# A graph network's node matrix as one float32r product of 258 columns, b2 read from memory, and a new order of the steps

## The chip, the cores and the metric

The kernel runs on one core of a Trainium2 chip. The metric is the device time of one launch in microseconds (us). The engines are named as the profile names them: PE (TensorE, matrix products; PEld is its loading of weights), DVE (VectorE), ACT (ScalarE), POOL (GpSimd) and SP, whose queue issues most DMAs. Each engine runs its own instructions in the order in which they were written.

## The reference

There are 128 graphs of 128 nodes with 512 features. For each graph, `adj` is a 128 x 128 matrix. Two layers follow one another; only what this case touches is shown in full.

```python
# layer 0: h = relu(layernorm(x));  x = x + (hconv(layernorm(relu(hconv(h, adj, W1, b1))), adj, W2, b2) + h)
def hypergraph_conv(x, adj, W, b):
    H = (adj != 0).astype(x.dtype)
    w = adj.reshape(N, -1)[:, :C]                    # adj's first row
    xw = jnp.einsum('ncd,hd->nch', x, W)
    Dn = jnp.einsum('nce,ne->nc', H, w)
    Dn = jnp.where(Dn > 0, 1.0 / Dn, 0.0)
    Be = H.sum(axis=1)
    Be = jnp.where(Be > 0, 1.0 / Be, 0.0)
    m = Be[:, :, None] * jnp.einsum('nce,nch->neh', H, xw)
    out = Dn[:, :, None] * jnp.einsum('nce,neh->nch', H, m)
    return out + b
# layer 1: h = relu(layernorm(x));  agg = adj @ h / max(row sums of adj, 1e-6)
#          x = x + relu(concat(h, agg) @ W.T)
```

All is float32. The hidden width of layer 0 is 1024 (W1 is 1024 x 512, W2 is 512 x 1024).

## The kernel before

A graph's 128 nodes lie on the 128 partitions. The H ... B ... H^T of the hypergraph convolution is one 128 x 128 **node matrix** per graph, S = H diag(1/Be) H^T, and the same product yields Dn, because the weights w (adj's first row) stand beside the scaled H as one more column. `incidence` transposes adj by blocks on DVE (`adjt`), writes the weight column into `sb`, turns adjt into zeros and ones while counting them, and takes the reciprocal of the count; `incidence_scale` writes the 128 scaled columns into `sb`; `node_matrix` (L402 to L408) multiplies `adjt` by `sb`, 128 x 129 columns in plain float32, and ACT evicts the sum to `s`; `node_scale` (L411 to L420) makes 1/Dn and its multiples from the last column, in four or five DVE instructions of one column (tile `dinv`).

The large products are made in float32r, which the program feeds with operands split in two parts: a high part `h` (a copy rounded down by a factor) and a low part `l` (the difference), and a third part `d` for a correction. `product` (L480 to L496) therefore runs three sweeps into two PSUM banks, called main (`rm`, `gm`, `bm`, `am`) and correction (`rd`, `gd`, `bd`, `ad`). Per graph these are conv1 in two halves (tiles `rm`, `rd`, twice), conv2 (`gm`, `gd`), the mean part of layer 1 (`bm`, `bd`) and its self part (`am`, `ad`). Small products are `ps_s` (node matrix), `pz` (conv1's nodes, float32), `ym` and `yd` (conv2's nodes, split as well) and the aggregation (L791).

The program is a software pipeline: `head` starts it, `step(s)` runs for s = 3 to 124, and `tail` ends it. Within a step the calls stand in an order written out by hand in the source, and every stage names its graph relative to s: `node_matrix(s + 1)`, `conv1_weights(s, 1)`, `conv2_nodes(s - 2)`, `layer1_mean(s - 3)` and so on. Nothing else schedules: an engine's queue is this order, filtered by engine. "Steady" graphs (3 to 120) take some other forms than those of head and tail.

Names used later. `conv1_out` (L514, DVE) adds a correction bank to `r`; `conv1_bias` (L519, POOL, pieces of 256 columns at L81) adds b1; `inner_*` is the layer norm of 1024 columns; `inner_out` and `inner_in` write r to DRAM and read it back in blocks (`n_scratch`, `nb`), `inner_turn` (L550) transposes the blocks into `nt`, which is split into `nh`, `nl`, `nd`. `layer1_trip_out`, `layer1_trip_in`, `layer1_turn`, `layer1_high`, `layer1_low`, `layer1_rest` do the same for layer 1 (`h_scratch`, `hb`, `ht`, `hh`, `hl`, `hd`). `mean_operator`, `mean_scale`, `mean_out`, `mean_in`, `mean_transpose` normalise adj by its row sums, and take it through DRAM (`an_scratch`, `anb`). `residual` (L436) adds h to x on POOL and then, for a steady graph, adds b2 with an accumulating DMA that POOL issues (`moved`, L91), from a copy of b2 on all partitions (`b2_bc`). `conv2_out` (L713) adds `ym` and `yd` to x. `scales` and `shifts` are the one-column instructions of the layer norms. Many tiles have one buffer: `r`, `adj`, `sb`, `ht`.

Of the kernel before, what the change touches and what calls it, by code (L numbers as in the profile page):

```python
# [24 lines left out]
def gnn_kernel(  # L25
# [34 lines left out]
    P = 128  # L60
# [99 lines left out]
    b2_bc = const.tile([P, D], FP, name="b2_bc")  # L160
# [171 lines left out]
    SB, HT, S, DN, H0, Z, PZ, SPLIT = ({} for _ in range(8))  # L332

    @stage
    def mean_operator(g):

        a = ADJ.pop(g)
        deg = small.tile([P, 1], FP, tag="deg", name="deg", bufs=2)
        nc.vector.tensor_reduce(deg, a, AX.X, ADD)
        nc.vector.tensor_scalar(deg, deg, EPS_DEG, 1.0 / 4096.0, MAX, MUL)  # L340
        nc.vector.reciprocal(deg, deg)
        ADJ[g] = a, deg
# [37 lines left out]
    @stage  # L380
    def incidence(g):


        HT[g] = at = pool.tile([P, P], FP, tag="ht", name="adjt")
        nc.vector.transpose(at, ADJB.pop(g))
        SB[g] = sb = small.tile([P, P + 1], FP, tag="sb", name="sb")
        nc.vector.tensor_scalar(sb[:, P : P + 1], at[:, 0:1], DOWN_12, None, MUL)
        cnt = small.tile([P, 1], FP, tag="cnt", name="cnt", bufs=2)
        nc.vector.tensor_scalar(at, at, 0.0, None, ALU.not_equal, ADD, accum_out=cnt)

        nc.vector.tensor_scalar(cnt, cnt, 1.0, None, MAX)
        nc.vector.reciprocal(cnt, cnt)
        SB[g] = sb, cnt

    @stage
    def incidence_scale(g, eng):
        SB[g], cnt = SB[g]
        scaled(eng, SB[g][:, :P], HT[g], cnt)


    @stage
    def node_matrix(g):  # L402
        ps = small_bank("ps_s")
        nc.tensor.matmul(ps[:, : P + 1], HT.pop(g), SB.pop(g), start=True, stop=True)  # L404
        s = small.tile([P, P + 1], FP, tag="s", name="s", bufs=4)
        copy(s, ps[:, : P + 1], AF.Copy, scale=4096.0 if steady(g) else 1.0)  # L406
        S[g] = s[:, :P]
# [3 lines left out]
    def node_scale(g):  # L411
        w = DN[g]
        DN[g] = dn = small.tile([P, 4], FP, tag="dinv", name="dinv", bufs=6)
        inv = dn[:, 2:3]
        nc.vector.tensor_scalar(inv, w, TINY, None, MAX)
        nc.vector.reciprocal(inv, inv)
        nc.vector.scalar_tensor_tensor(dn[:, 0:1], w, 0.0, inv, ALU.is_gt, MUL)
        nc.vector.tensor_scalar(dn[:, 1:2], dn[:, 0:1], ONE_UP, None, MUL)
        if not steady(g):
            nc.vector.tensor_scalar(dn[:, 3:4], dn[:, 0:1], DOWN_12, None, MUL)  # L420
# [15 lines left out]
    def residual(g, eng=nc.gpsimd):  # L436
        combine(eng, X[g], X[g], H0[g], ADD)
        if steady(g):
            moved(X[g], b2_bc)
        else:  # L440
            combine(eng, X[g], X[g], b2_bc, ADD)
# [373 lines left out]
    def step(s):  # L815
        node_high(s - 2)
        layer1_high(s - 3)
        conv2_bias(s - 2)
        inner_out(s - 1)
        inner_in(s - 1)  # L820
        conv2_high(s - 2)
        node_rest(s - 2)
        node_matrix(s + 1)
        mean_out(s - 3)
        layer1_low(s - 3, nc.vector)
        layer1_self_main(s - 4)
        conv1_weights(s, 1)
        mean_in(s - 3)
        conv2_low(s - 2, nc.vector)
# [3 lines left out]
        finish(s - 4)  # L833
        load_adj(s - 2)
        layer1_rest(s - 3)
        x_norm(s + 1)
        conv1_main(s, 0)
        conv2_out(s - 2)
        store(s - 4)
        conv1_nodes(s + 1)  # L840
        conv1_main(s, 1)
        conv1_out(s, 1)
        conv1_out(s, 0)
        conv1_high(s + 1)
        conv1_bias(s, 1)
        layer1_mean(s - 3)
        inner_turn(s - 1)
        layer1_sums(s - 2)
        conv1_bias(s, 0)
        conv1_low(s + 1)  # L850
        layer1_self(s - 3)
        layer1_mean_main(s - 3)
        layer1_spread(s - 2)
        load_adjb(s + 3)
        inner_high(s - 1)
        scales(s - 2, 3)
        mean_transpose(s - 3)
        shifts(s - 2, 3, nc.gpsimd)
        layer1_norm(s - 2)
        inner_sums(s)  # L860
# [583 lines left out]
```

## Time and profile before

| | us |
|---|---|
| median of 3 runs | 2458.57 (2458.56 to 2460.13) |
| the profiled execution | 2458.89 |
| its span, first to last instruction | 2457.1 |
| PE busy | 2437.2 (99%) |
| DVE busy | 2340.8 (95%) |
| ACT busy | 2061.8 (84%) |
| POOL busy | 1016.1 (41%) |

A span is what the instructions cover; 1.8 us lie around it. Busy shares are of the span. In lists of groups, the columns are line, engine, operation, tiles (output <- inputs), shape and count, then busy time in us, mean ns of one, and the engine's idle time just before with what ended it. In a list of one tile the columns are line, engine, operation, count, then the shortest, median and longest duration in ns. In a timeline they are start in us, duration in us, engine, line, operation, tiles; rows of a run of equal instructions are merged (x2, x4). In the chain, the columns are start, length and work.

### The profile page before, as it was taken

The page shows a single profiled execution, that of the slowest core. Times are in us where ns is not written, and L with a number is a line of the kernel's source. Part 1 is how long each engine was busy: PE and PEld are TensorE (multiplying, and loading weights), DVE is VectorE, ACT ScalarE, POOL GpSimd, SP SyncE. Part 2 cuts the span into 40 slices and gives each one's busy share as a digit, 9 for nine tenths or more (in the row PEclk, how much of TensorE's full clock was granted, in tenths as well). Part 3 has the DMA queues.
Part 4 walks back from the last instruction along what each step waited for, and adds up shares of the span by engine and source line. Part 5 has one row for each costly group of instructions (what it writes and reads, how often), then busy time and mean ns, then how long its engine had stood idle before and what let it go on. Part 6 is the DMA issues. An engine that isn't in the chain of part 4 may idle for free.

```text
span 2457.1 us, 41143 instructions
## 1 busy us (share of the span) xinstructions
PE 2437.2 (99%) x11300; PEld 2023.8 (82%) x11300; DVE 2340.8 (95%) x5358; ACT 2061.8 (84%) x4494; POOL 1016.1 (41%) x1560
## 2 busy tenths in 40 slices
PE   8999999999999999999999999999999999999998
PEld 6788888888888888888888888888888888888886
DVE  8899999999999999999999999999999999999987
ACT  8888888888888888888888888888888888888885
POOL 5434343444344434443444434343434343434452
PEclk9999999999999999999999999999999999999999
DMA  7454554445444544454455444544554454445432
GB/s 193 132 139 136 141 143 139 136 142 146 136 137 140 149 135 138 139 150 132 139 144 145 136 138 142 143 136 138 144 141 137 138 146 139 136 138 145 127 121 94
DMA packets 425943, 342.30 MB, mean 139 GB/s; under 512 B 178544, under 2 KB 341872, under 8 KB 425712
## 3 DMA queue, kind: packets, MB, share of 16 engines
q1 hardware_dynamic: 407888, 308.66, 41.0%
q0 software_dynamic: 17248, 30.95, 7.2%
q8 instruction: 89, 1.46, 0.3%
q14 instruction: 142, 1.16, 0.2%
q10 hardware_dynamic: 576, 0.07, 0.0%
HBM read 166.21 MB, written 142.34 MB: 126 GB/s over the span
## 4 chain that ended last, share of the span: by engine, by line
PE 83%; DVE 12%; issue 2%; ACT 2%; DMA 1%; SPq 0%; POOL 0%; DVEq 0%; ACTq 0%; POOLq 0%
PE gm L489 16%; PE rm L489 16%; PE bm L489 8%; PE am L489 8%; PE gd L494 8%; PE rd L494 8%; PE bd L494 4%; PE ad L494 4%; PE pz L447 4%; PE am L791 2%; PE ad L791 1%; DVE r L514 1%; PE ps_s L404 1%; PE yd L703 1%; PE ym L701 1%
## 5 line engine op out<-in xcount | busy, mean ns | idle before, releaser
L81 POOL TENSOR_TENSOR r<-r,b_bc 128x256 f32<-128x256 f32 x500 | 355.5, 743 | 772.5 <-DVE r L514 481.4
L303 POOL TENSOR_SCALAR st<-st 128x1 f32<-128x1 f32 x252 | 76.1, 302 | 566.9 <-DVE st L320 566.9
L460 ACT ACTIVATE z<-pz 128x512 fp32r<-128x512 f32 x128 | 76.5, 598 | 206.3 <-PE pz L447 206.3
L329 ACT ACTIVATE r<-r,st 128x1024 f32<-128x1024 f32 x128 | 159.3, 1244 | 76.7 <-POOL st L303 76.6
L81 POOL TENSOR_TENSOR g<-g,c 128x256 f32<-128x256 f32 x246 | 211.1, 1019 | 3.8 <-DVE g L653 3.8
L329 ACT ACTIVATE h<-x_t,st 128x512 f32<-128x512 f32 x255 | 206.2, 809 | 1.1 <-DVE st L303 0.4
L81 POOL TENSOR_TENSOR x_t<-x_t,h 128x256 f32<-128x256 f32 x256 | 184.7, 742 | 5.8 <-ACT h L329 5.8
L314 ACT ACTIVATE h<-x_t,st 128x512 f32<-128x512 f32 x255 | 183.5, 720 | 4.1
L514 DVE SCALAR_TENSOR_TENSOR r<-rd,dinv,r 128x512 f32<-128x512 f32 x256 | 179.8, 742 | 3.7 <-ACT r L509 1.8
L309 ACT ACTIVATE h<-x_t 128x512 f32<-128x512 f32 x255 | 159.5, 626 | 8.4 <-DVE x_t L713 5.5
L509 ACT ACTIVATE r<-rm,dinv 128x512 f32<-128x512 f32 x256 | 162.2, 690 | 4.2 <-PE rm L489 4.1
L550 DVE STREAM_TRANSPOSE nt<-nb 128x1024 f32<-128x1024 f32 x127 | 156.8, 1235 | 2.5 <-DMA nb<-n_scratch 2.5
L580 DVE SCALAR_TENSOR_TENSOR nd<-nh,nl 128x1024 fp32r<-128x1024 f32 x127 | 154.8, 1219 | 0.0
L81 DVE TENSOR_TENSOR nl<-nt,nh 128x1024 fp32r<-128x1024 f32 x126 | 152.2, 1208 | 0.0
L489 PE MATMUL rm<-w11h,z 128*128 128x512 f32 x512 | 152.0, 418 | 0.0
L489 PE MATMUL bm<-w30h,hh 128*128 128x512 f32 x504 | 146.9, 413 | 0.1
L447 PEld LDWEIGHTS pz<-s,h 128*128 128x128 f32 x1024 | 134.4, 192 | 13.7 <-ACT s L406 1.8
L314 ACT ACTIVATE junk<-r,st 128x1024 bf16<-128x1024 f32 x128 | 145.1, 1134 | 0.1
L489 PE MATMUL rm<-w11l,z 128*128 128x512 f32 x512 | 138.2, 392 | 0.0
L494 PE MATMUL rd<-w11d,z 128*128 128x512 f32 x512 | 138.0, 391 | 0.0
L447 PE MATMUL pz<-s,h 128*128 128x128 f32 x1024 | 135.9, 276 | 1.9 <-ACT s L406 1.3
L489 PE MATMUL rm<-w10h,z 128*128 128x512 f32 x512 | 137.7, 391 | 0.0
(240 smaller groups left out, 7527.0 us busy)
## 6 DMA issues: line engine op xcount, KB each, us to landing
n_scratch<-r SPq DMA_DIRECT2D x128, 512.0 KB, 2.6
nb<-n_scratch SPq DMA_DIRECT2D x508, 128.0 KB, 2.8
x_t<-in_x_dram SPq DMA_DIRECT2D x128, 256.0 KB, 2.8
h_scratch<-h SPq DMA_DIRECT2D x127, 256.0 KB, 2.0
hb<-h_scratch SPq DMA_DIRECT2D x508, 64.0 KB, 2.0
out_dram<-o SPq DMA_DIRECT2D x127, 256.0 KB, 2.1
x_t<-b_bc POOLq DMA_DIRECT2D x118, 256.0 KB, 3.7
adj_t<-in_adj_dram SPq DMA_DIRECT2D x128, 64.0 KB, 2.0
```

Of the source, the lines that this page charges most:

```text
L81: eng.tensor_tensor(dst[:, s], a[:, s], b[:, s], op)
L309: copy(junk, src, func, accum_out=t[:, 0:1])
L314: copy(junk, src, AF.Square, bias=t[:, 1:2], accum_out=t[:, 2:3])
L329: copy(dst, src, func, bias=t[:, 5:6], scale=t[:, 4:5])
L447: nc.tensor.matmul(z[:, k * P : (k + 1) * P], H0[g][:, k * P : (k + 1) * P], S[g], start=True, stop=True)
L460: copy(h, pz, AF.Copy, scale=DOWN)
L489: nc.tensor.matmul(pm, left[i](k), right(i, k), start=(i == 0 and k == 0), stop=(i == 1 and k == kk - 1))
L494: nc.tensor.matmul(pd, left[2](k), right(2, k), start=(k == 0), stop=(k == kk - 1), skip_group_check=True)
L509: copy(R[g][:, HALVES[half]], PY.pop((g, half)), AF.Copy, scale=DN[g][:, 1:2])
L514: nc.vector.scalar_tensor_tensor(r, PR.pop((g, half)), dn[:, 0:1], r, MUL, ADD)
L550: nc.vector.transpose(nt.rearrange("p k (i b) -> p k i b", b=B), t.rearrange("p i k a -> p k i a"))
L580: nc.vector.scalar_tensor_tensor(t, h, 2.0**-12, low, MUL, SUB)
```

## The change

Four things change.

1. The node matrix becomes one float32r product of 258 columns. The row factor is split: the pair (w, 1/Be) is rounded down on ACT (`incidence_high`), DVE takes the difference, and both scale the 0/1 matrix, so that `sb` holds a high half of 129 columns and a low half of 129 columns side by side. ACT evicts the first half, and a new DVE instruction (`node_sum`) adds the second from PSUM. The raw transposed adj now has a tile of its own (`raw`).
2. b2 has no copy on the partitions: the accumulating DMA reads b2's row in DRAM for every partition, and does so for all graphs.
3. Stages that were one are now several (`mean_operator`, `incidence`, `node_scale`), with an engine to be named for some one-column instructions.
4. `head`, `step` and `tail` have a new order, in which some stages also name another engine. In `step`: `layer1_low` DVE to POOL, `incidence_scale` POOL to DVE (low half) and ACT (high half), `shifts(s - 2, 3)` POOL to DVE, and the one-column instructions `node_floor` and `mean_degree` DVE to POOL, the weight column DVE to ACT.

The diff, without the orders of `head` and `tail`:

```diff
@@ -157,7 +157,6 @@
     }
 
     b1_bc = const.tile([P, DH], FP, name="b1_bc")
-    b2_bc = const.tile([P, D], FP, name="b2_bc")
     c0 = const.tile([P, D], FP, name="c0")
     gb = const.tile([P, 2, KH], FP, name="gb")
     eps = const.tile([P, 1], FP, name="eps")
@@ -329,7 +328,7 @@
         copy(dst, src, func, bias=t[:, 5:6], scale=t[:, 4:5])
 
 
-    SB, HT, S, DN, H0, Z, PZ, SPLIT = ({} for _ in range(8))
+    SB, HT, S, DN, H0, Z, PZ, SPLIT, PS = ({} for _ in range(9))
 
     @stage
     def mean_operator(g):
@@ -337,9 +336,17 @@
         a = ADJ.pop(g)
         deg = small.tile([P, 1], FP, tag="deg", name="deg", bufs=2)
         nc.vector.tensor_reduce(deg, a, AX.X, ADD)
-        nc.vector.tensor_scalar(deg, deg, EPS_DEG, 1.0 / 4096.0, MAX, MUL)
+        ADJ[g] = a, deg
+
+    @stage
+    def mean_degree(g, eng):
+        deg = ADJ[g][1]
+        eng.tensor_scalar(deg, deg, EPS_DEG, 1.0 / 4096.0, MAX, MUL)
+
+    @stage
+    def mean_inverse(g):
+        deg = ADJ[g][1]
         nc.vector.reciprocal(deg, deg)
-        ADJ[g] = a, deg
 
     @stage
     def mean_scale(g, eng):
@@ -381,43 +388,79 @@
     def incidence(g):
 
 
-        HT[g] = at = pool.tile([P, P], FP, tag="ht", name="adjt")
-        nc.vector.transpose(at, ADJB.pop(g))
-        SB[g] = sb = small.tile([P, P + 1], FP, tag="sb", name="sb")
-        nc.vector.tensor_scalar(sb[:, P : P + 1], at[:, 0:1], DOWN_12, None, MUL)
-        cnt = small.tile([P, 1], FP, tag="cnt", name="cnt", bufs=2)
-        nc.vector.tensor_scalar(at, at, 0.0, None, ALU.not_equal, ADD, accum_out=cnt)
-
-        nc.vector.tensor_scalar(cnt, cnt, 1.0, None, MAX)
-        nc.vector.reciprocal(cnt, cnt)
-        SB[g] = sb, cnt
-
-    @stage
-    def incidence_scale(g, eng):
-        SB[g], cnt = SB[g]
-        scaled(eng, SB[g][:, :P], HT[g], cnt)
-
+        raw = pool.tile([P, P], FP, tag="raw", name="raw")
+        nc.vector.transpose(raw, ADJB.pop(g))
+        HT[g] = at = pool.tile([P, P], FP, tag="ht", name="adjt").bitcast(FR)
+        two = small.tile([P, 2], FP, tag="cnt", name="cnt", bufs=2)
+        nc.vector.tensor_scalar(at, raw, 0.0, None, ALU.not_equal, ADD, accum_out=two[:, 1:2])
+
+        SB[g] = two, raw
+
+    @stage
+    def incidence_weight(g, eng):
+        two, raw = SB[g]
+        scaled(eng, two[:, 0:1], raw[:, 0:1], DOWN_12)
+
+    @stage
+    def incidence_count(g, eng):
+        two = SB[g][0]
+        eng.tensor_scalar(two[:, 1:2], two[:, 1:2], 1.0, None, MAX)
+
+    @stage
+    def incidence_inverse(g):
+        two = SB[g][0]
+        nc.vector.reciprocal(two[:, 1:2], two[:, 1:2])
+
+    @stage
+    def incidence_high(g):
+        two = SB[g][0]
+        t = small.tile([P, 2 * P + 4], FP, tag="sb", name="sb")
+        SB[g] = sb = t.bitcast(FR)
+        h, l = sb[:, P : 2 * P + 3 : P + 2], sb[:, 2 * P + 1 : 2 * P + 4 : 2]
+        copy(h, two, AF.Copy, scale=DOWN)
+        nc.vector.tensor_tensor(l, two, h, SUB)
+        SPLIT["sb", g] = t[:, 2 * P + 2 : 2 * P + 3], t[:, 2 * P + 3 : 2 * P + 4]
+
+    @stage
+    def incidence_scale(g, i, eng):
+        c = SPLIT["sb", g][i]
+        scaled(eng, SB[g][:, i * (P + 1) : i * (P + 1) + P], HT[g], c)
 
     @stage
     def node_matrix(g):
-        ps = small_bank("ps_s")
-        nc.tensor.matmul(ps[:, : P + 1], HT.pop(g), SB.pop(g), start=True, stop=True)
+        PS[g] = ps = small_bank("ps_s")
+        nc.tensor.matmul(ps[:, : 2 * P + 2], HT.pop(g), SB.pop(g)[:, : 2 * P + 2], start=True, stop=True)
         s = small.tile([P, P + 1], FP, tag="s", name="s", bufs=4)
         copy(s, ps[:, : P + 1], AF.Copy, scale=4096.0 if steady(g) else 1.0)
+        S[g] = s
+
+    @stage
+    def node_sum(g):
+        s = S[g]
+        nc.vector.scalar_tensor_tensor(s, PS.pop(g)[:, P + 1 : 2 * P + 2], 4096.0 if steady(g) else 1.0, s, MUL, ADD)
         S[g] = s[:, :P]
         DN[g] = s[:, P : P + 1]
 
     @stage
-    def node_scale(g):
+    def node_floor(g, eng):
         w = DN[g]
         DN[g] = dn = small.tile([P, 4], FP, tag="dinv", name="dinv", bufs=6)
-        inv = dn[:, 2:3]
-        nc.vector.tensor_scalar(inv, w, TINY, None, MAX)
-        nc.vector.reciprocal(inv, inv)
-        nc.vector.scalar_tensor_tensor(dn[:, 0:1], w, 0.0, inv, ALU.is_gt, MUL)
-        nc.vector.tensor_scalar(dn[:, 1:2], dn[:, 0:1], ONE_UP, None, MUL)
+        eng.tensor_scalar(dn[:, 2:3], w, TINY, None, MAX)
+        DN[g] = dn, w
+
+    @stage
+    def node_scale(g):
+        DN[g], w = DN[g]
+        dn = DN[g]
+        nc.vector.reciprocal(dn[:, 2:3], dn[:, 2:3])
+        nc.vector.scalar_tensor_tensor(dn[:, 0:1], w, 0.0, dn[:, 2:3], ALU.is_gt, MUL)
+
+    @stage
+    def node_up(g, eng):
+        dn = DN[g]
+        scaled(eng, dn[:, 1:2], dn[:, 0:1], ONE_UP)
         if not steady(g):
-            nc.vector.tensor_scalar(dn[:, 3:4], dn[:, 0:1], DOWN_12, None, MUL)
+            scaled(eng, dn[:, 3:4], dn[:, 0:1], DOWN_12)
 
     @stage
     def x_sums(g, tag="B"):
@@ -435,10 +478,7 @@
     @stage
     def residual(g, eng=nc.gpsimd):
         combine(eng, X[g], X[g], H0[g], ADD)
-        if steady(g):
-            moved(X[g], b2_bc)
-        else:
-            combine(eng, X[g], X[g], b2_bc, ADD)
+        moved(X[g], b2.partition_broadcast(P))
 
     @stage
     def conv1_nodes(g):
@@ -814,591 +854,661 @@
 
     def step(s):
         node_high(s - 2)
+        mean_out(s - 3)
+        conv2_bias(s - 2)
+        load_adj(s - 2)
+        node_rest(s - 2)
+        conv2_high(s - 2)
         layer1_high(s - 3)
-        conv2_bias(s - 2)
-        inner_out(s - 1)
-        inner_in(s - 1)
-        conv2_high(s - 2)
-        node_rest(s - 2)
         node_matrix(s + 1)
-        mean_out(s - 3)
-        layer1_low(s - 3, nc.vector)
+        layer1_low(s - 3)
+        conv2_low(s - 2, nc.vector)
+        mean_operator(s - 2)
+        node_sum(s + 1)
+        conv1_weights(s, 1)
         layer1_self_main(s - 4)
-        conv1_weights(s, 1)
-        mean_in(s - 3)
-        conv2_low(s - 2, nc.vector)
         layer1_self_out(s - 4)
         conv2_rest(s - 2)
         conv2_nodes(s - 2)
-        finish(s - 4)
-        load_adj(s - 2)
+        conv1_main(s, 0)
+        node_floor(s + 1, nc.gpsimd)
+        inner_out(s - 1)
+        inner_in(s - 1)
         layer1_rest(s - 3)
         x_norm(s + 1)
-        conv1_main(s, 0)
         conv2_out(s - 2)
-        store(s - 4)
         conv1_nodes(s + 1)
         conv1_main(s, 1)
+        layer1_sums(s - 2)
+        layer1_mean(s - 3)
+        mean_in(s - 3)
+        layer1_spread(s - 2)
         conv1_out(s, 1)
+        finish(s - 4)
+        layer1_mean_main(s - 3)
+        conv1_bias(s, 1)
+        store(s - 4)
+        inner_turn(s - 1)
+        mean_degree(s - 2, nc.gpsimd)
+        load_adjb(s + 3)
         conv1_out(s, 0)
-        conv1_high(s + 1)
-        conv1_bias(s, 1)
-        layer1_mean(s - 3)
-        inner_turn(s - 1)
-        layer1_sums(s - 2)
+        inner_high(s - 1)
         conv1_bias(s, 0)
-        conv1_low(s + 1)
-        layer1_self(s - 3)
-        layer1_mean_main(s - 3)
-        layer1_spread(s - 2)
-        load_adjb(s + 3)
-        inner_high(s - 1)
         scales(s - 2, 3)
+        shifts(s - 2, 3, nc.vector)
+        layer1_norm(s - 2)
         mean_transpose(s - 3)
-        shifts(s - 2, 3, nc.gpsimd)
-        layer1_norm(s - 2)
-        inner_sums(s)
         layer1_mean_out(s - 3)
         layer1_mean_high(s - 3)
+        node_scale(s + 1)
+        layer1_self(s - 3)
+        load_x(s + 2)
         inner_low(s - 1, nc.vector)
-        mean_rest(s - 3)
+        layer1_mean_low(s - 3, nc.vector)
+        layer1_trip_out(s - 2)
         inner_rest(s - 1)
-        layer1_mean_low(s - 3, nc.vector)
+        inner_sums(s)
+        inner_spread(s)
         layer1_mean_rest(s - 3)
-        inner_spread(s)
         scales(s, 2)
+        mean_inverse(s - 2)
         shifts(s, 2, nc.gpsimd)
         conv2_weights(s - 1)
-        layer1_trip_out(s - 2)
+        mean_rest(s - 3)
+        incidence(s + 2)
+        conv1_high(s + 1)
+        conv2_main(s - 1)
+        mean_scale(s - 2, nc.scalar)
+        incidence_count(s + 2, nc.vector)
+        conv1_low(s + 1)
+        inner_norm(s)
+        layer1_trip_in(s - 2)
+        incidence_weight(s + 2, nc.scalar)
+        x_sums(s + 2)
+        incidence_inverse(s + 2)
+        conv2_weights_out(s - 1)
+        conv1_rest(s + 1)
+        incidence_high(s + 2)
         residual(s + 1)
-        incidence(s + 2)
-        inner_norm(s)
+        x_spread(s + 2)
+        layer1_turn(s - 2)
         aggregate(s - 3)
-        node_scale(s + 1)
-        load_x(s + 2)
-        mean_operator(s - 2)
-        conv2_main(s - 1)
-        layer1_trip_in(s - 2)
-        conv2_weights_out(s - 1)
-        x_sums(s + 2)
-        x_spread(s + 2)
-        mean_scale(s - 2, nc.scalar)
-        conv1_rest(s + 1)
-        layer1_turn(s - 2)
-        incidence_scale(s + 2, nc.gpsimd)
+        incidence_scale(s + 2, 1, nc.vector)
+        incidence_scale(s + 2, 0, nc.scalar)
+        scales(s + 2, 1)
         conv1_weights(s + 1, 0)
-        scales(s + 2, 1)
         shifts(s + 2, 1, nc.vector)
+        node_up(s + 1, nc.vector)
...
```

## The prediction

> **What bounds the kernel now.** I read the busy shares first (PE 99%, DVE 95%), then the busy time in windows, which is alike from 100 us to 2300 us, so one step stands for 118 steady graphs. In the window from 1000 to 1500 us:
>
> ```profile
> 1000.00:1500.00 500.00, 500.00 (x2333) 417.60 (x2332) 484.05 (x1121) 424.26 (x932) 206.06 (x319) 1.00 0.49 141
> ```
>
> PE has no gap in 500 us at a granted clock of 1.00. Next the chain that ended last, two steps of it:
>
> ```profile
> 1216.58 0.22 PE ps_s L404 x2
> 1216.80 1.85 PE rm L489 x8
> 1218.65 0.92 PE rd L494 x4
> 1219.57 0.23 PE ym L701
> ...
> 1220.25 0.89 PE pz L447 x8
> 1221.14 1.83 PE bm L489 x8
> ...
> 1226.60 3.63 PE gm L489 x16
> ...
> 1235.44 0.22 PE ps_s L404 x2
> ...
> 1238.43 0.23 PE ym L701
> ```
>
> The reader sees PE alone, matmul after matmul. A step is 1238.43 - 1219.57 = 18.86 us. A float32r matmul of 512 columns takes 3.63 / 16 = 0.227; the node matrix, float32 with 129 columns, appears as two records of 0.11. PE is the bound.
>
> But DVE is close behind, so I read its timeline beside POOL's (POOL last, and one tile's list):
>
> ```profile
> 1212.28 0.17 DVE L416 RECIPROCAL dinv<-dinv 128x1 f32<-128x1 f32 x1
> 1212.48 0.39 DVE L417 SCALAR_TENSOR_TENSOR dinv<-s,dinv 128x1 f32<-128x1 f32 x1
> ...
> 1215.77 0.51 DVE L682 SCALAR_TENSOR_TENSOR sp<-sp,s 128x128 fp32r<-128x128 f32 x1
> 1216.20 0.28 DVE L683 SCALAR_TENSOR_TENSOR sp<-sp,s 128x128 fp32r<-128x128 f32 x1
> 1216.40 0.68 DVE L81 TENSOR_TENSOR hl<-ht,hh 128x512 fp32r<-128x512 f32 x1
> 1217.01 0.68 DVE L81 TENSOR_TENSOR gp<-g,gp 128x512 fp32r<-128x512 f32 x1
> ```
> ```profile
> 1211.42 1.43 POOL L81 TENSOR_TENSOR x_t<-x_t,h 128x256 f32<-128x256 f32 x2
> ...
> 1214.39 1.73 POOL L81 TENSOR_TENSOR g<-g,c 128x256 f32<-128x256 f32 x2
> ```
> ```profile
> L417 DVE SCALAR_TENSOR_TENSOR dinv<-s,dinv x128: 159/391/401, 20.7 to 2396.5; 128x1 f32<-128x1 f32 x128
> ```
>
> DVE instructions follow one another with no wait worth naming. Two are long for their size: L417 takes 0.39 where 0.159 is possible, and ends (1212.87) with POOL's x_t (1212.85); L682 takes 0.51 where its twin L683 takes 0.28, and ends just after POOL's g (1216.12). Both read two tiles in SBUF while POOL reads two there. I call this a **meeting**; a step before has two, 0.46 us in all.
>
> **The change part by part.** *Node matrix on PE.* Removed: 0.22. Added: one float32r matmul of 258 columns, 258/512 of 0.227 = 0.114. Bounds: 0.11 (one float32 record of half the width) and 0.227 (it might take as long as 512 columns). I take 0.114, since float32r time is set by columns in every row here that I can scale. PE loses 0.11 per step: 18.75. The eight matmuls behind a float32 product take 1.85, those among float32r 1.81; another 0.04 may go, not counted.
>
> *DVE's own work*, in distances from start to start. Removed: hl 0.61 (to POOL), the weight column L387 0.19, L415 0.17 and L340 0.18: 1.15. Moved apart: before, bl and the bd that reads it stand 0.80 apart, where two independent instructions of that size stand 0.61 apart: 0.20 saved. Three one-column results (L391, L417, L340) are no longer read by the next instruction, which costs 0.19 where an independent one costs 0.08: 0.3. Added: the low pair (128 x 2) 0.19, as a one-column instruction, bounds 0.16 and 0.39 from L417; the low half's scale 0.29 (same shape on DVE at 9.03 us); node_sum, 129 columns from PSUM, 0.30, between L683's 0.28 and L682's 0.51; one shift 0.21. Sum 0.99. Net -0.66. Own work is 18.86 - 0.46 (meetings) - 0.66 = 17.74, leaving 1.0 us per step under PE's 18.75 for meetings.
>
> *Meetings in the new order.* From the order of DVE and POOL I find four: dinv's product with conv1_bias(s, 0); the anp splits with shifts(s, 2); the low pair with conv2_bias; gp or the third part of g (L730) with hl, new on POOL (two pieces of 0.74, the row of r's bias there). Lower bound 0 each (the partner can be early), upper 0.55 (DVE's r<-r,b_bc took 1247 ns against 693 once in the tail). I take somewhat under the rows' 0.23, 0.18 each: 0.7, inside the 1.0. So hl's move costs nothing while DVE has this room; without it, all of it counts.
>
> [...]
>
> *ACT* gains the weight column and the high pair (0.20 each, as L310) and the high half's scale (0.39, as L301): 0.8. It is busy 424 of 500, 16.0 of 18.86 us, and stays under 17. *POOL* loses sb's scale (0.91) and a shift (0.28) and gains hl (1.48) and two one-column instructions (0.3 each): 206/500 x 18.86 = 7.8 becomes 8.7. Its conv1 bias starts behind `finish`, which now follows the first conv1_out and reads two SBUF tiles: up to 0.68 later, ahead of inner_sums, which ACT reaches some 0.5 later still.
>
> *b2's read.* Per transfer the same bytes. Issued at 1213.15, used by ym at 1220.06; it lands after 3.7 (median), so 3 us are free. A row of b2 read for all partitions at the start took 7.6, among loads of the same size that took 6.7 and 8.7 there; that is their queue, and I count 0. The other end, 7.6 - 6.9 = 0.7 per step, goes to the range. In head and tail 20 POOL pieces (17 us) go, off PE's path.
>
> *The queue of SP.* The new order puts r's way out (`inner_out`) behind adj's. Rows before:
>
> ```profile
> 1212.76 0.34 SPq L535 DMA_DIRECT2D n_scratch<-r  x1
> 1215.40 1.76 SPq L543 DMA_DIRECT2D nb<-n_scratch  x4
> 1217.26 0.38 SPq L535 DMA_DIRECT2D an_scratch<-adj_t  x1
> ...
> 1221.50 0.43 SPq L290 DMA_DIRECT2D adj_t<-in_adj_dram  x1
> ```
>
> From gm's end: g's eviction 0.58, adj's scale 0.39, an_scratch lands 2.5 later, only then may adj's one buffer be loaded (issue 0.43), then n_scratch lands 2.6 later and frees r's one buffer for ACT's rm (0.69), then x_norm (0.81) for pz: 8.0, with six hand-overs of 0.05 (1215.40 behind a landing at 1215.36) 8.3. PE reaches pz 1220.25 - 1211.37 - 0.11 = 8.8 after gm's end, and reads it 0.16 earlier: 0.3 spare. nb lands about 0.5 ahead of `inner_turn`. An issue is now and then 1 us late (the adj load took 1.46 at 1202.75); I put 0.02 per step for that.
>
> *Sum*, against the profiled execution (2458.9, 0.3 above the median): 118 x (0.11 - 0.02) = 10.6, ten other graphs x 0.11 = 1.1, head and tail otherwise 0 with 4 either way: 2447.2.
>
> **The rivals.** (1) *DVE becomes the bound through meetings* (slower). It decides where meetings exceed 18.86 - 17.74 = 1.1 per step. At 0.32 each, 1.28: DVE 19.02, +0.16 x 118 = 2478. For it: hl adds two POOL pieces among gp and L730. Against: deg, node_sum and o, which stand between these two, read PSUM or one tile.
> (2) *SP's longer chain stops PE before pz.* 0.3 is spare; at 0.5 late, PE loses 0.2 per step: 18.95, 2469. For it: each landing is a median, and two stand in series. Against: ACT's waits now lie elsewhere.
> (3) *No gain*: 258 columns cost as much as 512, 0.227 against 0.22, or head and tail lose what the steps gain: 2459.
>
> **How the numbers follow.** My forecast 0.58 (own range 2440 to 2453), rival 1 0.17, rival 2 0.13, rival 3 0.12. A measurement of this kernel tells 0.2% (4.9 us) from no change. Faster: nearly all of the forecast and a little of rivals 2 and 3, 0.60. Within 0.2%: 0.15, mostly rival 3. Slower: 0.25. Low end 2440: the 0.04 behind the product and 4 from head and tail; high end 2482 takes in rival 1 at its price.
>
> **What would show it.** Right: ps_s one record per graph, the next matmul 0.11 behind it; ym to ym 18.75; DVE still with no long wait, or a short one before ym; L420 and L434 on ACT without pushing pz. Wrong: idle time of PE before yd (L730 late), before pz (h or s late), or before ps_s; DVE instructions of two SBUF tiles at twice their length; ACT waiting for n_scratch before r; DVE waiting for x_t's DMA from b2.

## The result and the profile after

The changed kernel takes 2572.76 us (median of 4 runs, 2571.52 to 2575.37), the kernel before 2458.57 in the same comparison: a ratio of 1.0464, 95% interval 1.0446 to 1.0483. The change costs 114 us, where 12 us of gain were forecast.

I read first the page of the profile after (busy shares, the chain that ended last, the DMA issues with their size and median time to landing):

```profile
span 2571.2 us, 41753 instructions
...
PE 2497.2 (97%) x11170; PEld 1989.8 (77%) x11170; DVE 2369.4 (92%) x5372; ACT 2137.3 (83%) x4872; POOL 1256.2 (49%) x1787
...
PE 41%; ACT 20%; DMA 18%; DVE 11%; issue 7%; SPq 3%; POOL 0%; DVEq 0%; ACTq 0%; POOLq 0%
...
n_scratch<-r SPq DMA_DIRECT2D x128, 512.0 KB, 4.5
nb<-n_scratch SPq DMA_DIRECT2D x508, 128.0 KB, 2.8
...
x_t<-in_b_dram POOLq DMA_DIRECT2D x128, 256.0 KB, 4.4
h_scratch<-h SPq DMA_DIRECT2D x127, 256.0 KB, 2.5
...
adj_t<-in_adj_dram SPq DMA_DIRECT2D x128, 64.0 KB, 3.2
```

The same lines of the page before:

```profile
PE 83%; DVE 12%; issue 2%; ACT 2%; DMA 1%; SPq 0%; POOL 0%; DVEq 0%; ACTq 0%; POOLq 0%
...
n_scratch<-r SPq DMA_DIRECT2D x128, 512.0 KB, 2.6
...
x_t<-b_bc POOLq DMA_DIRECT2D x118, 256.0 KB, 3.7
adj_t<-in_adj_dram SPq DMA_DIRECT2D x128, 64.0 KB, 2.0
```

Before, PE was 83% of the chain and DVE 12%. Now PE is 41%, ACT 20% and transfers 18%. One landing stands out: n_scratch, r's way out, takes 4.5 us from its issue and took 2.6 before; adj's load takes 3.2 and took 2.0. Neither PE nor DVE is fuller than before: PE's share fell from 99% to 97%, DVE's from 95% to 92%.

The groups of instructions (busy time, mean ns of one, then the idle time before them and what ended it) say who waits:

```profile
L549 ACT ACTIVATE r<-rm,dinv 128x512 f32<-128x512 f32 x256 | 174.2, 682 | 156.1 <-DMA n_scratch<-r 126.6 <-DVE o L837 11.7 <-DVE s L440 11.6
...
L590 DVE STREAM_TRANSPOSE nt<-nb 128x1024 f32<-128x1024 f32 x127 | 158.0, 1244 | 68.0 <-DMA nb<-n_scratch 59.1 <-issue 8.4
...
L421 DVE TENSOR_TENSOR sb<-cnt,sb 128x2 fp32r<-128x2 f32 x128 | 143.1, 1118 | 9.3 <-ACT sb L420 5.0
...
L487 PEld LDWEIGHTS pz<-s,h 128*128 128x128 f32 x1024 | 126.5, 192 | 53.4 <-ACT h L328 49.3 <-PE pc L264 1.6 <-issue 0.5
L81 DVE TENSOR_TENSOR gp<-g,gp 128x512 fp32r<-128x512 f32 x118 | 117.6, 996 | 0.4
```

ACT stands 127 us for n_scratch (r has one buffer) and DVE 59 us for nb, which is read back from n_scratch. PE's weight loads for pz wait 49 us for ACT's h, which comes behind r; before, this wait was 1.0 us. The rows of L421 and gp are meetings: the subtraction of the low pair (L421), two columns wide, takes 1.12 us where its shortest took 0.15, and gp 1.00 where it took 0.68.

So there are two suspects, and the trace alone does not tell which of them holds the other up. The timeline of SP's queue and the chain show how the first would work:

```profile
1212.28 0.34 SPq L575 DMA_DIRECT2D an_scratch<-adj_t  x1
1213.82 0.35 SPq L289 DMA_DIRECT2D adj_t<-in_adj_dram  x1
1214.26 0.38 SPq L575 DMA_DIRECT2D n_scratch<-r  x1
1218.73 1.74 SPq L583 DMA_DIRECT2D nb<-n_scratch  x4
```
```profile
1257.88 2.72 DMA n_scratch<-r
...
1260.68 0.69 ACT r L549
1261.37 0.71 ACT h L328
...
1262.12 1.16 PE pz L487 x8
...
1281.20 4.01 DMA nb<-n_scratch
...
1285.34 1.26 DVE nt L590
...
1286.62 1.07 ACT nh L611
```

Followed through one step of the trace, this is a **loop**: gm's end, g's eviction (ACT, 1211.36), adj's scale (1211.86 to 1212.25), an_scratch lands (1213.80), adj's load, n_scratch issued (1214.26) and landed (1218.66), nb's four reads (the last lands at 1224.38), nt (1224.50 to 1225.75), nh (1225.78 to 1226.84), gm (1226.89 to 1231.06), and g's eviction again at 1231.56: 20.2 us in that step. What goes round in a loop sets the period, whatever the engines could do. With n_scratch landing in 2.6 it would be 18.4, under PE's 18.75.

The round has a second way, and in most steps that is the one that holds: in 15 of 102 steady steps gm starts within 0.12 us of nh's end, and in the others PE is then still at the work before it, late from pz. From gm's end n_scratch's landing takes 8.0 us, r and h up to pz another 1.6, PE's own work from pz to gm 6.5, and gm 3.7 (means of the steady steps): 19.8. Both ways pass n_scratch's landing.

Why it lands late can be seen in the pieces of the transfers, which the trace records with their starts. In the step above, b2's transfer is issued by POOL at 1213.32, and its 128 pieces of 2 KB start between 1215.05 and 1216.88. The 128 pieces of 4 KB of n_scratch, issued at 1214.26, start between 1216.37 and 1218.14: behind b2's. The first piece moves 2.1 us behind the issue (median), where it was 0.84 before.

The time per step, from the first ym to the last, is 19.791 us, and 18.867 before: 117 x 0.924 = 108 us. The first ym stands 3.4 us later (110.0 for 106.6), and the span ends 145.7 us behind the last ym and not 143.0, 2.7 more. The sum is 114, that of the result.

### The profile page after: what moved, and what is told of

It reads as the page before. It is cut to its first block, busy times and chain, and to the rows that moved or that the text cites. A ratio compares the mean times of both kernels' runs of the same rounds, so it can differ in the third digit from the quotient of the medians.

```text
span 2571.2 us, 41753 instructions
## 1 busy us (share of the span) xinstructions
PE 2497.2 (97%) x11170; PEld 1989.8 (77%) x11170; DVE 2369.4 (92%) x5372; ACT 2137.3 (83%) x4872; POOL 1256.2 (49%) x1787
## 4 chain that ended last, share of the span: by engine, by line
PE 41%; ACT 20%; DMA 18%; DVE 11%; issue 7%; SPq 3%; POOL 0%; DVEq 0%; ACTq 0%; POOLq 0%
PE gm L529 9%; DMA n_scratch<-r 8%; DMA nb<-n_scratch 6%; PE rm L529 6%; PE bm L529 5%; PE am L529 5%; ACT r L328 3%; PE pz L487 3%; PE gd L534 3%; PE rd L534 3%; PE bd L534 3%; SPq L583 2%; PE ad L534 2%; ACT nh L611 2%; DVE nt L590 2%
## 5 line engine op out<-in xcount | busy, mean ns | idle before, releaser
L81 POOL TENSOR_TENSOR r<-r,b_bc 128x256 f32<-128x256 f32 x502 | 407.1, 832 | 522.7 <-DVE r L554 406.8
L81 POOL TENSOR_TENSOR hl<-ht,hh 128x256 fp32r<-128x256 f32 x248 | 228.3, 940 | 202.2 <-ACT hh L611 202.1
L549 ACT ACTIVATE r<-rm,dinv 128x512 f32<-128x512 f32 x256 | 174.2, 682 | 156.1 <-DMA n_scratch<-r 126.6
L302 POOL TENSOR_SCALAR st<-st 128x1 f32<-128x1 f32 x127 | 56.6, 445 | 462.2 <-DVE deg L349 449.2
L81 POOL TENSOR_TENSOR g<-g,c 128x256 f32<-128x256 f32 x246 | 201.1, 941 | 1.3 <-DVE g L693 0.6
L611 ACT ACTIVATE nh<-nt 128x1024 fp32r<-128x1024 f32 x127 | 134.3, 1058 | 51.5 <-DVE nt L590 50.6
L487 PE MATMUL pz<-s,h 128*128 128x128 f32 x1024 | 145.5, 285 | 18.9 <-ACT h L328 16.9
L421 DVE TENSOR_TENSOR sb<-cnt,sb 128x2 fp32r<-128x2 f32 x128 | 143.1, 1118 | 9.3 <-ACT sb L420 5.0
L529 PE MATMUL gm<-w20l,nl 128*128 128x512 f32 x508 | 139.9, 397 | 2.6 <-DVE nl L81 0.2
L529 PE MATMUL gm<-w20h,nh 128*128 128x512 f32 x508 | 138.6, 395 | 2.0 <-ACT nh L611 1.6
```

Of the source, the lines that this page charges most:

```text
L81: eng.tensor_tensor(dst[:, s], a[:, s], b[:, s], op)
L487: nc.tensor.matmul(z[:, k * P : (k + 1) * P], H0[g][:, k * P : (k + 1) * P], S[g], start=True, stop=True)
L529: nc.tensor.matmul(pm, left[i](k), right(i, k), start=(i == 0 and k == 0), stop=(i == 1 and k == kk - 1))
L549: copy(R[g][:, HALVES[half]], PY.pop((g, half)), AF.Copy, scale=DN[g][:, 1:2])
L611: copy(h, a, AF.Copy, scale=DOWN)
```

## The experiments

Unless the text says otherwise, a kernel is the changed one with one edit. The table has the time per step from ym to ym, the median landing of n_scratch behind its issue, the time, and the ratio to the kernel before measured beside it.

| run | us per step | n_scratch lands in | us | ratio, 95% interval |
|---|---|---|---|---|
| before | 18.867 | 2.6 | 2458.6 | |
| after | 19.791 | 4.5 | 2572.8 | 1.0464 (1.0446 to 1.0483) |
| e1_sp | 22.040 | 3.4 | 2848.0 | 1.1582 (1.1565 to 1.1600) |
| e2_low | 19.773 | 4.7 | 2568.5 | 1.0445 (1.0430 to 1.0461) |
| e3_both | 22.091 | 3.2 | 2846.7 | 1.1583 (1.1564 to 1.1603) |
| e6_b2only | 18.881 | 2.6 | 2460.9 | 1.0009 (0.9999 to 1.0018) |
| e7_b2late | 18.843 | 2.7 | 2461.2 | 1.0007 (0.9998 to 1.0016) |
| e8_b2late_low | 18.850 | 2.7 | 2463.1 | 1.0015 (1.0005 to 1.0024) |
| e9_sp2 | 20.282 | 2.7 | 2632.0 | 1.0700 (1.0683 to 1.0716) |
| e10_all | 18.778 | 2.7 | 2457.7 | 0.9993 (0.9984 to 1.0003) |
| e11_order | 19.510 | 2.9 | 2541.8 | 1.0339 (1.0322 to 1.0357) |
| e13_b2sbuf | 19.346 | 3.9 | 2525.5 | 1.0270 (1.0256 to 1.0284) |
| e15_ht | 18.787 | 2.7 | 2465.4 | 1.0028 (1.0017 to 1.0040) |
| e16_b2sbuf_all | 18.727 | 2.8 | 2453.6 | 0.9983 (0.9975 to 0.9992) |
| e17_b2sbuf_low | 19.094 | 3.9 | 2494.5 | 1.0147 (1.0130 to 1.0164) |
| e18_filler | 18.849 | 2.7 | 2461.8 | 1.0013 (1.0003 to 1.0022) |
| e19_hl | 19.265 | 2.8 | 2514.6 | 1.0229 (1.0213 to 1.0244) |
| e20_filler2 | 18.797 | 2.7 | 2459.6 | 1.0007 (0.9997 to 1.0017) |

### The low pair in another form (e2_low)

```diff
-        nc.vector.tensor_tensor(l, two, h, SUB)
+        for i, c in enumerate((P, 2 * P + 2)):
+            nc.vector.tensor_scalar(l[:, i : i + 1], two[:, i : i + 1], t[:, c : c + 1], None, SUB)
```

> The changed kernel with the low pair as two one-column instructions that take the high part as a per-partition operand, in the same place on DVE; nothing else. Theory B (meetings): each of the two takes about 0.2 us, DVE gets 0.8 us per step back, and the time falls by 0.6 to 0.9 x 118 to 2465 to 2500 us. Theory A (SP's order): DVE waits that much longer for nb, 2555 to 2573 us. If the two wait for POOL as the one did, nothing changes in the trace either.

Measured: 2568.5 us, as theory A said. The groups of this run:

```profile
L591 DVE STREAM_TRANSPOSE nt<-nb 128x1024 f32<-128x1024 f32 x127 | 158.2, 1245 | 111.6 <-DMA nb<-n_scratch 105.4 <-issue 6.1
...
L488 PEld LDWEIGHTS pz<-s,h 128*128 128x128 f32 x1024 | 125.1, 192 | 113.0 <-ACT h L328 110.2 <-PE pc L264 1.6 <-issue 0.7
...
L81 DVE TENSOR_TENSOR gp<-g,gp 128x512 fp32r<-128x512 f32 x118 | 81.4, 690 | 2.0
...
L422 DVE TENSOR_SCALAR sb<-cnt,sb 128x1 fp32r<-128x1 f32 x256 | 42.8, 209 | 6.5 <-ACT sb L420 3.2
```

Both meetings are gone: 0.21 us for each of the two instructions in place of 1.12, and gp back at 0.69. From start to start the two places give DVE 1.1 us per step back; some of it goes at once to the low half's scale just behind (0.46 us where it took 0.26), and DVE is busy 93 us less in the whole run, 0.8 per step. It spends them waiting: for nb 105 us where it was 59, for adj 55 where it was 20. The step did not move: PE, whose idle time before ps_s falls from 36 us to 6, now waits for h before pz instead (110 us where it was 49). So the meetings were real, and were not what set the step. It also shows what this meeting hung on: the same subtraction, on the same engine at the same place, took 0.21 us a column and not 1.12 for the two once its second input came in as a per-partition operand and not as a second tile.

### SP's order (e1_sp, e3_both and e9_sp2)

```diff
     def step(s):
         node_high(s - 2)
+        inner_out(s - 1)                 # e1_sp
         mean_out(s - 3)
+        inner_out(s - 1)                 # e9_sp2 has it here
         conv2_bias(s - 2)
         load_adj(s - 2)
+        inner_in(s - 1)
...
-        inner_out(s - 1)
-        inner_in(s - 1)
```

> The changed kernel with r's way out (`inner_out`) issued ahead of adj's (`mean_out`, `load_adj`) in a step and its way back (`inner_in`) behind them; nothing else. Theory A (SP's order: DVE's 0.52 us per step for nb and ACT's wait for n_scratch set the step): both waits go, the step falls by 0.5 to 0.9 us, 2465 to 2515 us. Theory B (DVE meetings set the step: the low pair's subtraction takes 1.08 us instead of 0.19 and gp 0.94 instead of 0.63, so DVE's own work is about 19.0): the waits go but DVE is full, the step stays at 19.3 to 19.8, 2520 to 2573 us. Theory C (b2's read from memory makes landings slow): n_scratch still lands 4.4 us after its issue; by A and B about 2.6.

e3_both is e1_sp with e2_low's edit.

> The changed kernel with both edits of the two runs before. Theory A: no better than the SP order alone by more than 0.3 per step (35 us). Theory B: no better than the low pair alone by more than 35 us. If the two hold each other up in one loop (DVE late makes r late, which makes nb late), neither alone gives its whole share and both together reach the 2447 us of the forecast within 10 us.

> The changed kernel, b2's transfer where the change put it, with SP's order an_scratch, n_scratch, adj's load, nb (r's way out no longer behind an_scratch's landing). Theory D (the loop through SP sets the step): n_scratch is issued as soon as r is normalised, 0.5 to 0.8 us earlier, beside b2's transfer rather than behind it, and every step is shorter by that and by what the landing gains: 2450 to 2515 us. If the loop is not what counts, 2555 us or more, or worse where adj's load comes late, as in e1_sp.

Measured: 2848, 2847 and 2632 us. The first two missed every range by far; e9_sp2 went the way of its last clause, with adj's load late. (The granted clock of e1_sp and e3_both was 0.97; of the 16% by which they are slower that is 3 at most.) The group of deg in e1_sp, and two DMA issues of e9_sp2:

```profile
L338 DVE TENSOR_REDUCE deg<-adj_t 128x1 f32<-128x128 f32 x128 | 36.5, 285 | 335.4 <-DMA adj_t<-in_adj_dram 335.4
```
```profile
n_scratch<-r SPq DMA_DIRECT2D x128, 512.0 KB, 2.7
...
adj_t<-in_adj_dram SPq DMA_DIRECT2D x128, 64.0 KB, 5.2
```

nb came in time (DVE waits 5.0 us for it in e1_sp, 3.6 in e9_sp2, and 59 in the changed kernel), so the order did what it was to do for r. But adj's way was as tight: the new order has `mean_operator` early in the step, right behind adj's load. In e1_sp an_scratch, issued 0.4 us behind n_scratch, landed after 4.6 us and not 1.5, and later than b2's transfer in 85 of 90 steps; in e9_sp2 adj's load landed after 5.2 us and not 3.2 (one was issued at 1204.31, inside b2's transfer, which landed at 1209.56; adj's 64 KB landed at 1209.78). n_scratch itself, issued 0.2 us behind b2 there and not 1.1, landed in 2.7, its pieces ahead of b2's. What was issued well behind or inside b2's 256 KB came late, and an order that spared n_scratch put adj there instead. Whether b2's transfer is the cause was tested next.

### b2's transfer out of the way (e7_b2late, e8_b2late_low, e10_all)

```diff
-        moved(X[g], b2.partition_broadcast(P))
+        if not steady(g):
+            moved(X[g], b2.partition_broadcast(P))
+
+    @stage
+    def residual_bias(g):
+        if steady(g):
+            moved(X[g], b2.partition_broadcast(P))
...
         conv1_bias(s, 0)
+        residual_bias(s)
```

> The changed kernel with b2's accumulating DMA taken out of `residual` in the steady graphs and issued one step later, behind conv1_bias(s, 0) on POOL, some 6 us before r's way out instead of 0.9 us before it. Theory D (a loop of one step through SP: gm, g's eviction, adj's scale, an_scratch's landing, adj's load, n_scratch, nb, nt, nh, gm; it is too long because n_scratch, issued just behind b2's transfer, lands 4.5 us after its issue and not 2.6): n_scratch lands in 2.6 to 3.0 us, DVE's wait for nb goes, and the step falls to what DVE needs with its meetings, 18.75 to 18.95: 2447 to 2475 us. Theory E (n_scratch is slow for another reason, adj's or hb's transfers): still 4 us and more, 2560 to 2573 us.

Measured: 2461.2 us. Of the 114 us, 112 went with one DMA issued elsewhere. The page of this run:

```profile
PE 90%; DMA 4%; ACT 3%; DVE 1%; issue 1%; SPq 1%; POOL 0%; DVEq 0%; ACTq 0%; POOLq 0%
...
n_scratch<-r SPq DMA_DIRECT2D x128, 512.0 KB, 2.7
```

n_scratch lands in 2.7, its first piece 0.90 us behind the issue (0.84 before, 2.1 in the changed kernel), PE is 90% of the chain, and most steps take 18.747 us, the forecast's 18.75. The mean is 18.843: 12 of 117 steps are over 19.2 us, and the same waits, for n_scratch and nb, are what is left (19 and 9 us in the whole run). b2's own transfer did not get faster (5.2 us); it only no longer stands ahead of r's.

e8_b2late_low adds e2_low's edit, and e10_all adds e9_sp2's order on SP to that:

> The same with the low pair as two one-column instructions (e2_low's edit). Theory D: the loop is short and DVE needs only 18.0 us, so PE is the bound again at 18.75: 2445 to 2455 us, no more than 25 us under e7_b2late. Theory E: 2555 to 2570 us, as e2_low.

> The same as e8_b2late_low, and on SP r's way out stands between adj's way out and adj's load (an_scratch, n_scratch, adj's load, nb), so that n_scratch need not wait for an_scratch's landing. Theory D: n_scratch is issued 0.8 us earlier and the loop is 0.8 us shorter still; where PE is the bound already this buys nothing, 2445 to 2455 us. If adj's load, behind two issues, comes late for deg, DVE waits for adj and the time is above 2470 us.

Measured: 2463.1 and 2457.7 us, 8 and 3 us over the ranges. Taking out what is left of the low pair's meeting bought nothing here either. But e8_b2late_low is the clean pair to e2_low: neither has the long meeting, they differ by b2's place alone, and that is worth 105 us (2568.5 to 2463.1). The order that lost 59 us in e9_sp2 now gains 5: with b2's transfer gone, adj's load and n_scratch both land in time, and only 2 steps are over 19.2 us. Its step of 18.778 is 0.09 under before, 10 us in 117 steps, but its total is level with before: the rest went in head and tail (first ym at 109.1 and not 106.6, 147.5 us of span behind the last ym and not 143.0).

### b2's read alone, and b2 from SBUF in the new order (e6_b2only, e13_b2sbuf, e17_b2sbuf_low)

e6_b2only is the kernel before with `moved(X[g], b2.partition_broadcast(P))` in place of `moved(X[g], b2_bc)`.

> The kernel before with b2's row read from memory in the steady graphs, and nothing else. By theory C n_scratch and x_t land later (4 us and more after the issue) and the time is above 2480 us. By theories A and B landings stay as before (n_scratch 2.6, x_t 3.7) and the time is 2455 to 2463 us.

Measured: 2460.9 us, within what can be told from before. Yet the read is not free. The DMA issues of this run:

```profile
n_scratch<-r SPq DMA_DIRECT2D x128, 512.0 KB, 2.6
nb<-n_scratch SPq DMA_DIRECT2D x508, 128.0 KB, 3.5
...
x_t<-in_b_dram POOLq DMA_DIRECT2D x118, 256.0 KB, 5.1
...
an_scratch<-adj_t SPq DMA_DIRECT2D x128, 64.0 KB, 3.2
```

b2's transfer takes 5.1 us and took 3.7 from SBUF; nb, issued behind it, lands in 3.5 (2.8 before), an_scratch in 3.2 (2.5). In the old order n_scratch is issued 0.4 us ahead of b2 and does not feel it, and the others have room.

e13_b2sbuf asks the opposite: the new order, with b2 in SBUF again.

```diff
+    b2_bc = const.tile([P, D], FP, name="b2_bc")
...
-        raw = pool.tile([P, P], FP, tag="raw", name="raw")
+        raw = pool.tile([P, P], FP, tag="ant", name="raw")
...
-        t = small.tile([P, 2 * P + 4], FP, tag="sb", name="sb")
+        t = pool.tile([P, 2 * P + 4], FP, tag="anb", name="sb")
...
-        moved(X[g], b2.partition_broadcast(P))
+        moved(X[g], b2_bc)
...
```

> The changed kernel with b2's row in SBUF again (raw shares ant's place and sb shares anb's to make room; mean_in(0) in the head and incidence_high of the last graph in the tail stand a few stages later for it), same place of b2's DMA. If reading one row of memory for all partitions is what makes b2's transfer long (5.1 us in e6_b2only against 3.7) and what stands behind it late, n_scratch lands in 3.0 to 3.6 us and the step falls to 18.75 to 19.1: 2450 to 2490 us. If the place behind b2's transfer does it, whatever the source, n_scratch lands in 4.2 us or more: 2540 to 2573 us.

Measured: 2525.5 us, between the two answers. By these times the source of b2 is worth 47 of the 114 us, and its place another 64 (to e7_b2late). n_scratch lands in 3.9, behind a transfer of 3.6 (4.4 in the changed kernel). In this run DVE waits little, and its meetings are longer still (L422, the low pair, 1.17 us; gp 1.13), so whether the loop or the meetings held it was open. e17_b2sbuf_low takes the low pair's meeting out (e2_low's edit):

> e13_b2sbuf with the low pair as two one-column instructions. In e13_b2sbuf DVE's work with its meetings is 18.95 of 19.35 us and n_scratch lands in 3.9. If the loop through n_scratch holds e13_b2sbuf, the DVE time gained turns into waits for nb and g as in e2_low, and the step stays at 19.1 to 19.35: 2500 to 2525 us. If the meetings hold it, the step falls to 18.75 to 18.95: 2450 to 2478 us.

Measured: 2494.5 us, just under the range for the loop. The groups:

```profile
L592 DVE STREAM_TRANSPOSE nt<-nb 128x1024 f32<-128x1024 f32 x127 | 157.9, 1244 | 53.5 <-DMA nb<-n_scratch 52.8
...
L81 DVE TENSOR_TENSOR gp<-g,gp 128x512 fp32r<-128x512 f32 x118 | 81.3, 689 | 1.7
...
L423 DVE TENSOR_SCALAR sb<-cnt,sb 128x1 fp32r<-128x1 f32 x256 | 42.7, 209 | 4.3 <-ACT sb L421 3.3
```

DVE is busy 97 us less in the whole run. The wait for nb takes 38 of them (53 us where it was 15), smaller waits the rest but for 0.25 us per step, so at a landing of 3.9 the meetings count for 31 us. The three kernels without the low pair's meeting and with SP's order as changed put the loop plainly: n_scratch in 2.7, 3.9, 4.7 us gives steps of 18.85 (PE needs 18.75), 19.09 and 19.77.

### The meeting put back (e18_filler, e20_filler2)

In e7_b2late POOL no longer issues b2's DMA just ahead of g's bias, and the low pair's meeting shrank as well (L421 0.36 us on average). To part the two, an idle POOL instruction went where the DMA issue had stood, once and then twice:

```diff
+    idle = const.tile([P, P], FP, name="idle")
+    nc.vector.memset(idle, 1.0)
...
+        if steady(g):
+            nc.gpsimd.tensor_scalar(idle, idle, 1.0, None, MUL)
```

> e7_b2late with an idle POOL instruction (128x128, result unused) where b2's DMA was issued, so that g's bias on POOL stands as late as in the changed kernel and meets the low pair on DVE again, while n_scratch has nothing ahead of it. If the loop alone makes the loss, 2455 to 2470 us, as e7_b2late, even with the low pair at 1.0 us and more. If moving the meeting was what helped e7_b2late, 2500 us or more. If both count where DVE is nearly full (17.96 us without, some 19.0 with the meetings), the step is 18.9 to 19.1: 2465 to 2495 us.

> e18_filler with the idle POOL instruction twice (2 x 0.54 us; once, g's bias on POOL still waited 0.32 for DVE's g and the low pair took only 0.29). Now g's bias begins some 0.2 us after g is ready, as in the changed kernel, and the low pair should take 1.0 us and more again, with n_scratch landing in 2.7. If the loop alone makes the loss: 2455 to 2470 us. If the meeting costs its 0.9 us on its own: 2520 us or more. If DVE's 18.0 us without meetings leave room up to 18.75, 18.8 to 18.95 per step: 2460 to 2480 us.

Measured: 2461.8 and 2459.6 us; but the low pair took 0.35 us in the steady part of both, so the long meeting did not come back, although in e20_filler2 g's bias no longer waited for g. What these two runs tell is that a later POOL cost nothing here (e7_b2late took 2461.2), so the loss came from b2's transfer and not from the time that POOL spends on issuing it. A long meeting at the low pair was seen where b2's DMA issue stands directly ahead of g's bias in the new order and the old form is kept (after, e1_sp, e9_sp2, e13_b2sbuf: 0.78 to 1.17 us). What that issue has to do with it stays open, and so does what the meeting would cost at a landing of 2.7.

### The product in the old order (e11_order)

> The changed kernel's product and b2's read from memory, head and tail as changed, but the step in the order of before (hl on DVE, r's way out ahead of adj's; the new instructions stand next to those that they belong to). If the loss lies in the new order (theories A and D), it is gone: n_scratch lands in 2.6 to 3.3 us; DVE, full before, has some 0.5 us more per step, so 2465 to 2520 us. If the product itself is what costs, 2540 us or more.

The edit: the changed kernel's stages in before's `step`, with `incidence_weight`, `incidence_count`, `incidence_inverse`, `incidence_high` behind `incidence`, `node_sum` behind `conv2_low`, hl on DVE. Measured: 2541.8 us, just inside the range for "the product itself". The waits for n_scratch and nb are gone (0.3 and 4.6 us in the whole run), and the chain that ended last is another:

```profile
DVE 72%; issue 10%; DMA 6%; PE 5%; SPq 3%; ACT 2%; DVEq 1%; POOL 0%; ACTq 0%; POOLq 0%
```

DVE was nearly full before, and the new instructions (the low pair 0.57, the low half's scale, node_sum) come on top, with 35 us of waiting for ACT's high pair: 19.51 us per step. So the product needs an order that frees DVE; the change's order did that, and lost it elsewhere.

### hl's move, and a version that beats both (e16_b2sbuf_all, e19_hl, e15_ht)

e16_b2sbuf_all is e10_all with b2 in SBUF as in e13_b2sbuf.

> e10_all with b2's row in SBUF. Theory D: the loop has room already, so a shorter transfer of b2 buys nothing in the steps: 2453 to 2460 us. Under 2452 us would mean that b2's read still costs in e10_all.

Measured: 2453.6 us, 0.17% faster than before (interval 0.08% to 0.25%), the only kernel here that beats both. Its first and last ym stand at 113.1 and 2304.1: 18.727 per step, no step over 19.2. PE is 95% of its chain. It gains 16 us in the steps and gives 9 back in head and tail, 6.5 of them before the first ym.

e19_hl is that kernel with `layer1_low(s - 3, nc.vector)`.

> e16_b2sbuf_all with hl back on DVE. DVE's work there is 18.16 us of 18.73; hl adds 0.61 and takes away L737's meeting with it (0.16): 18.6. If that holds, the step stays at 18.73 to 18.8 and the time at 2452 to 2464 us; if DVE's order leaves no room for it, the step rises by up to 0.6: up to 2525 us.

Measured: 2514.6 us, 61 us slower. By the sum of its work DVE had room. By its order it had not:

```profile
L81 DVE TENSOR_TENSOR hl<-ht,hh 128x512 fp32r<-128x512 f32 x123 | 85.1, 692 | 63.6 <-ACT hh L619 63.5
```

On DVE hl stands ahead of gp and waits 0.53 us per step for ACT's hh, and gp, L738 and yd wait behind it. So at this place in the new order hl's move to POOL was needed; another place on DVE was not tried.

e15_ht gives e10_all the head and tail of before, with the new instructions next to the old ones.

> e10_all's step (18.765 us) with head and tail in the order of before, the new product's instructions next to the old ones. If the new head and tail cost the 8 to 9 us by which e10_all misses 2447 (its first ym stands 2.5 us later than before's and its end 5 us later after the last ym), they come back: 2443 to 2451 us. If not, 2454 to 2460 us, as e10_all.

Measured: 2465.4 us, over both ranges. The steps stay at 18.787, and the first ym comes at 117.6, later than in any other run. What the new head (3.4 us) and the new tail (2.7) lose is not explained by that order, and is left open.

## Why the prediction was wrong

**The step that failed** is the queue of SP. I laid r's way out behind adj's, took the landing of n_scratch from before ("then n_scratch lands 2.6 later"), and got 8.3 us against 8.8, 0.3 to spare. The order of the hand-overs held; the landing measured 4.5, and pz started 9.6 us behind gm's end and not 8.8 (8.8 again in e10_all, where n_scratch lands in 2.7). The sum itself moved n_scratch to a later issue, and did not ask what would then be ahead of it: b2's transfer, issued at 1213.32 with n_scratch at 1214.26, where before n_scratch stood first (1212.76, b2 at 1213.15). With 4.5 for 2.6 (and 1.5 for an_scratch's 2.5) the same sum gives 9.2, 0.4 over PE's 8.8; most of the rest is g's eviction, which begins 0.3 behind gm's end.

I also followed the chain only to pz, as if the next step began afresh. It goes on to gm, by PE's own work in most steps and through nb, nt and nh in some, and so closes on itself. "nb lands about 0.5 ahead of `inner_turn`" was the sign of it: 0.5 us of slack in a loop, priced as a margin for a hiccup (0.02 per step).

**b2's read, counted at nothing.** For the time of the kernel before it was right (e6_b2only), for the transfers not: 5.1 us for 3.7, and 0.7 more for two that stand behind. I had looked for b2's row among loads at the start and taken the length for their queue. In the new order it is worth 47 us (e13_b2sbuf); my upper end of 0.7 per step, 83 us, would have held it, but it never got into the range: 2447 and 83 are 2530, and the range ended at 2482.

**Rival 2** (SP's longer chain) was the mechanism, and at pz, as it said: 0.8 of the 1.04 us that a step lost to the forecast's 18.75 lie between gm's end and pz, 0.1 between pz and gm, 0.1 in gm. I priced it at 0.2 per step. Both ends that I gave it came from landings of before.

**Meetings.** I forecast 0.7 us per step, at most 0.55 each. By the rows they came to 1.28: the low pair 0.89, gp 0.32, the rest 0.07. The bound of 0.55 failed at the low pair. DVE's own work is 17.9 us (in e8_b2late_low the step of 18.85 less 0.81 of gaps over 0.1 us and 0.17 by which L737 is long; forecast 17.74). In the changed kernel the step less such gaps is 18.7, so the meetings add 0.8 net to DVE's time, as instructions behind them moved closer. By the rows rival 1's condition (over 1.1) was met, by the net it was not; either way the kernel without meetings was no faster (e2_low). They count where the loop is shorter: 31 us at 3.9.

How long a meeting lasts is seen in the trace of the changed kernel. In 67 of 118 steps POOL's piece of hl starts 0.12 us ahead of gp, and gp takes 1.23 us and not 0.69: 0.55 more, where 0.68 of that piece was still to run. At the low pair the wait is longer than one instruction: it begins 0.43 us behind the first of POOL's two pieces of g and ends 0.03 behind the second (medians). In e7_b2late the low pair lost 0.2.

**The product** was right: one record per graph, the next matmul 0.114 to 0.118 us behind it where PE is the bound (forecast 0.114), and 18.747 per step in most steps of e7_b2late, e8_b2late_low and e10_all (forecast 18.75). Rival 3's 0.227 for 258 columns falls. Every float32r row before had 512 columns, so that the time goes with their number was my assumption there; here 258 of them took 258/512 of 0.227.

**Head and tail**, put at 0 within 4, lost 6.1.

**ACT and POOL** were no bound, as said. POOL's 8.7 us per step became 9.9: among others hl's pieces took 0.94 us and r's 0.83, where I had 0.74 for both.

What would have shown it was in the list: "ACT waiting for n_scratch before r" went from nothing to 127 us. The range ended at 2482, because every rival was priced with the durations of before.

## What to carry to other kernels

When a DMA is moved in an order, look up which transfers of other queues are under way at its new place, and do not take its landing from the old one (here 4.5 us at the new place, 2.6 at the old). When a chain through one-buffer tiles and DRAM comes back to the engine where it began, add up its whole round and compare it with the step: half a microsecond of slack in the loop was no margin here. Two suspects that both show in the profile are parted by removing one at a time: here removing 0.8 us per step of DVE time moved nothing, and moving one DMA moved 112 us.

## What the runs showed of the hardware

- A write of 512 KB to DRAM landed 2.6 to 2.8 us behind its issue with no accumulating transfer just ahead of it (before, e7_b2late, e16_b2sbuf_all), in 2.7 and 2.9 us when issued 0.2 us behind one (e9_sp2, e11_order), in 3.9 us when issued 1.0 us behind one of 256 KB from SBUF (3.6 us itself; e13_b2sbuf), and in 4.5 us when issued 1.1 us behind one from a single row of DRAM (the changed kernel). Short transfers suffered as much: adj's 64 KB, issued inside b2's transfer, landed with it, after 5.2 us (e9_sp2) where it took 3.2 in the changed kernel. There, in the step followed above, the pieces of b2 start 1.3 us ahead of n_scratch's. Why they go first no run shows: which engine moved which piece is not in the trace.
- Reading one row of 2 KB of DRAM for all 128 partitions, accumulating, took 4.4 to 5.7 us in the kernels shown, and the same bytes from SBUF 3.6 to 4.0; at the same place in the order 4.4 against 3.6 (new: the changed kernel, e13_b2sbuf), 5.1 against 3.7 (old: e6_b2only, before).
- The same subtraction of two columns on DVE took 1.12 us with two tiles as inputs beside POOL (the changed kernel), and 0.21 us per column with the second as a per-partition operand (e2_low).
